# Channel sums of the q and k norms by way of HBM, roots on GpSimd, value transposes in pairs: an attention and convolution kernel on one Trainium2 core

## Chip, cores, metric

The kernel runs on one NeuronCore of a Trainium2 chip. The metric is the device time of one launch in microseconds. Three runs of the kernel before gave 3830.28, 3835.93 and 3836.73 us, so the median is 3835.93 us. All data is float32.

## What is computed

The input x has 48 channels of 256 x 256 pixels. Two layers follow each other, each added to its input after a group norm. The first is attention over 4 x 4 patches, the second a sum of three small matrix products along width, height and channel within 64 x 64 windows. The change touches the first:

```python
qkv = jnp.einsum('bchw,oc->bohw', gn(x), w_qkv)
qkv = dwconv3x3(qkv, w_dw)
q, k, v = jnp.split(qkv, 3, axis=1)
q, k, v = (heads(q), heads(k), heads(v))   # unfold in 4x4 patches, 8 heads
q = q / max(sqrt(sum(q*q, axis=-2)), 1e-12)   # the sum runs over 96 = 6 channels x 16 pixels
k = k / max(sqrt(sum(k*k, axis=-2)), 1e-12)
attn = softmax(einsum('bhcn,bhcm->bhnm', q, k) * temperature)
out = einsum('bhcn,bhnm->bhcm', v, attn)
```

A head has 96 values for each of 4096 patches (plus border patches, which are zero and enter as a constant in the softmax sums). A patch's norm takes the squares of 6 channels and 16 pixels.

## The kernel before

Engines are named as in the profile: PE is TensorE, DVE VectorE, ACT ScalarE, POOL GpSimd, SP SyncE.

**Stages.** First x is loaded and its group statistics are taken. The 1x1 convolution of heads 0 and 1 follows (`pointwise`), then the depthwise convolution and norms of head 0 (`depthwise_first`). Then comes the attention of heads 0 to 7, in which the depthwise part of head h+1 runs beside the attention of head h. The projection and the second layer end the kernel. A branch for large temperatures (line 465) is not taken with these inputs.

**The attention loop** (lines 607 to 690) is under a manual schedule, so each engine issues its instructions in the order of the program text. For each head h there are 16 steps g, called stages here, and in each stage four steps k. A stage computes two blocks of 128 rows of scores (`scores`: 24 PE products of 512 columns and four exponentials on ACT for each block), normalises them on DVE (`normalised`: four small operations that end in the scaled value tile vn), and weighs the values with them (`weigh`, line 563: four groups of products, k = 0 to 3). Each group is added to the accumulator oacc by DVE (line 581). Scores, weighted sums and the strips named below take turns in three PSUM tiles named big.

**The depthwise rows.** In stages g = 0 to 11 of heads 0 to 6, ten rows r = 0 to 9 of the next head pass through (`Depthwise`, line 199). A tile has 126 partitions: 7 chunks of the image times 18 channels (6 each of q, k and v). Row d = g - 1 is handled thus in stage g. DVE runs taps 1 to 3 after the first `normalised`, taps 4 to 8 after the second (`tap`, line 234). ACT squares the result (`square`, line 245). At k=0 DVE sums the 16 pixels (`reduce`, line 249, result ss, 126 x 64). At k=2 a PE product with a 0/1 matrix named same adds the 6 channels of a group and leaves the sum in each of their partitions (`norm`, line 253, result pn in PSUM), and DVE computes the inverse root of it by an integer guess and three Newton steps, twelve operations in all (`root`, lines 257 to 274, result y; q rows are multiplied by the temperature, v rows become 1). At k=3 DVE multiplies the row by y (`scale`, line 279, result o).

In the following stage the row is p = g - 2. POOL stores o, ACT rounds o to oh, POOL subtracts to get ol (`low`, line 292), and POOL stores both (line 297). Row n = g gets its first tap on ACT (`first`, line 215). In head 0 each step k also has a strip of the 1x1 convolution of heads 2 to 7 (`Strip`: a load, four PE products, one ACT pass, two stores).

**SP's queue** issues, in the order of the text: values and keys of the next head, the queries of stage g+2, in head 0 the strips' loads and stores, and at k=2 the `pad` tile of row g+1.

**Value transposes.** In stages g = 11 to 14 of heads 0 to 6, `load_value` fetches two value tiles of the next head through SP (two buffers vt). `turn` (line 521) transposes one tile by four PE transposes into a PSUM tile pst, and ACT copies it to vT. One turn is at k=0, the other at k=2. pst shares two PSUM buffers, tag "one", with pn and with the output transposes pt.

Of the kernel before, what the change touches and what calls it, by code (L numbers as in the profile page):

```python
# [8 lines left out]
F32 = mybir.dt.float32  # L9
F32R = mybir.dt.float32r  # L10
AF = mybir.ActivationFunctionType
ALU = mybir.AluOpType
AX = mybir.AxisListType
# [16 lines left out]
CR = 9  # L30
HC = 3 * C // NH
NP1 = CH * HC
PX = W // KS
# [10 lines left out]
def conv_preact_kernel(  # L44
# [15 lines left out]
    nc = tc.nc  # L60
# [4 lines left out]
    dram = ctx.enter_context(tc.tile_pool(name="dram", bufs=1, space=DRAM))  # L65
# [6 lines left out]
    CN = CR * PX  # L72
    t1 = [dram.tile([(h1 - h0) * HC, TR, W + 2], F32, name=f"t1_{h0}") for h0, h1 in GROUPS]
    qkv = [dram.tile([3, CH, HC * KK, CN + PX], F32, name=f"qkv{h}") for h in range(NH)]
    os_ = dram.tile([C * KK, NT], F32, name="os_")
    x1s = dram.tile([C, H, W], F32, name="x1s")

# [15 lines left out]
    for s in range(2):  # L93
        r = slice(s * C, (s + 1) * C)
        for h in range(NH if s == 0 else H0):
            o = s * M0 + h * HC if h < H0 else (h - H0) * HC
            nc.scalar.dma_start(
                out=(wq[r] if h < H0 else wr[0:C])[:, o : o + HC].rearrange("c (z e) -> c z e", z=3),
                in_=w_qkvT.rearrange("c (z h e) -> h c z e", z=3, h=NH)[h],
# [4 lines left out]
    for z in range(3):  # L104
        for j in range(CH):
            p = j * HC + z * 6
# [23 lines left out]
    nmul = const.tile([NP1, NH], F32, name="nmul")  # L130
    nadd = const.tile([NP1, 1], F32, name="nadd")
# [65 lines left out]
    class Depthwise:  # L197
# [53 lines left out]
        def norm(self):  # L251
            self.pn = one.tile([NP1, PX], F32, name="pn", tag="one")
            nc.tensor.matmul(self.pn, lhsT=same, rhs=self.ss, start=True, stop=True)  # L253

        def root(self, on_scalar=False):
            n = self.pool.tile([NP1, PX], F32, name="n", bufs=2)
            nc.vector.tensor_scalar_max(n, self.pn, 1e-24)
            y = self.pool.tile([NP1, PX], F32, name="y", bufs=2)
            if on_scalar:
                nc.scalar.activation(n, n, AF.Sqrt)  # L260
                nc.vector.reciprocal(y, n)
                nc.vector.tensor_scalar(y, y, nmul[:, self.h : self.h + 1], nadd, ALU.mult, ALU.add)
                self.y = y
                return

            nc.vector.tensor_scalar(
                y.bitcast(mybir.dt.int32), n.bitcast(mybir.dt.int32), -0.5, 1597463007.0, ALU.mult, ALU.add
            )
            z = self.pool.tile([NP1, PX], F32, name="z", bufs=self.bufs)
            for _ in range(3):  # L270
                nc.vector.tensor_mul(z, y, y)
                nc.vector.scalar_tensor_tensor(z, z, -0.5, n, ALU.mult, ALU.mult)
                nc.vector.scalar_tensor_tensor(y, z, 1.5, y, ALU.add, ALU.mult)
            nc.vector.tensor_scalar(y, y, nmul[:, self.h : self.h + 1], nadd, ALU.mult, ALU.add)
            self.y = y
# [112 lines left out]
    with tc.tile_pool(name="xn", bufs=1) as xnp, tc.tile_pool(name="cst", bufs=1) as cst, tc.tile_pool(  # L388
        name="nps", bufs=2, space=PSUM
# [9 lines left out]
        for j in range(0, HALF, LR):  # L399
            for s in range(2):  # L400
                eng = nc.sync if s == 0 else nc.scalar
                eng.dma_start(
                    out=xr[s * C : (s + 1) * C, j : j + LR, :], in_=xc[:, s * HALF + j : s * HALF + j + LR, :]
# [8 lines left out]
        for g, (w, k) in enumerate(((wq, P2), (wr, C))):  # L412
            m = w.shape[1]
# [51 lines left out]
    with tc.If(nc.values_load(large) > 0):  # L465
# [8 lines left out]
        with tc.tile_pool(name="mk", bufs=NM) as mk, tc.tile_pool(name="mq", bufs=2) as mq, tc.tile_pool(  # L474
            name="mps", bufs=2, space=PSUM
# [23 lines left out]
    with tc.tile_pool(name="ahead", bufs=2) as ah, tc.tile_pool(name="ae", bufs=3) as ae, tc.tile_pool(  # L499
        name="asm", bufs=6  # L500
# [6 lines left out]
        def load_key(h, m, eng=nc.sync):  # L507
            keys[h, m] = ah.tile([128, 2, 512], F32R, name="kt", bufs=14)
            load_keys(keys[h, m], h, m, eng)

        def load_query(h, g):
            queries[h, g] = ah.tile([128, 3, 256], F32R, name="qt", bufs=2)
            load_queries(queries[h, g], h, g)

        def load_value(h, m):

            vt = ah.tile([HD, 4 * 128], F32, name="vt")
            load(vt, qkv[h][2, :, 2 * HD :], m * 512, (m + 1) * 512)
            values[h, m] = vt

        def turn(h, m):
            ps = one.tile([128, 4, HD], F32, name="pst", tag="one")
            for i in range(4):
                nc.tensor.transpose(ps[:, i, :], values[h, m][:, i * 128 : (i + 1) * 128], ident[:HD, :HD])  # L524
            vT = ah.tile([128, 4, HD], F32, name="vT", bufs=9)
            nc.scalar.copy(vT, ps)
            values[h, m] = vT
# [79 lines left out]
        with tc.manual_schedule():  # L607
            load_query(0, 1)
            block = scores(0, 0)
            for h in range(NH):  # L610
                more = h + 1 < NH
                rows = {r: Depthwise(h + 1, r) for r in range(CR + 1)} if more else {}
                for g in range(NG):
                    p, d, n = rows.get(g - 2), rows.get(g - 1), rows.get(g)

                    if h == 0 and 0 < g <= 6:
                        load_value(0, g + 1)
                    if more and CR + 2 <= g < CR + 6:
                        for m in range(2):
                            load_value(h + 1, (g - CR - 2) * 2 + m)  # L620
                    if more and CR + 3 <= g < CR + 6:
                        for m in range(2):
                            load_key(h + 1, (g - CR - 3) * 2 + m)

                    blocks = [normalised(*block)]
                    block = scores(h, g * G + 1)
                    if more and g == NG - 1:
                        load_key(h + 1, 6)
                        load_key(h + 1, 7, nc.gpsimd)
                    if g + 2 < NG:  # L630
                        load_query(h, g + 2)
                    elif more:
                        load_query(h + 1, g + 2 - NG)
                    if p:
                        p.store((2,))
                    if d:
                        for t in range(1, 4):
                            d.tap(t)
                    second = block
                    if g + 1 < NG:  # L640
                        block = scores(h, (g + 1) * G)
                    elif more:
                        block = scores(h + 1, 0)
                    blocks.append(normalised(*second))
                    if d:
                        for t in range(4, 9):
                            d.tap(t)

                    if g == 0 and rows:
                        rows[0].load()  # L650
                    if p:
                        p.high()
                    if d:
                        d.square()
                    if n:
                        n.first()
                    for k in range(NK):
                        s = (h * NG + g) * NK + k
                        weigh(h, g, blocks, k)
                        if k == 0 and d:  # L660
                            d.reduce()
                        if k == 0 and p:
                            p.low(nc.gpsimd)
                            p.store((0, 1))
                        for w in strips[s]:
                            w.run(big.tile([128, 2, 512], F32, name="big"))
                        for w in strips[s + 2]:
                            w.load()
                        for w in strips[s - 1] if s else []:
                            w.store()  # L670
                        if k == 2 and d:
                            d.norm()
                            d.root()
                        if k == 2 and g + 1 in rows:
                            rows[g + 1].load()
                        if k == 3 and d:
                            d.scale()
                        if h == 0 and 0 < g <= 6 and k == 0:
                            turn(0, g + 1)
                        if more and CR + 2 <= g < CR + 6 and k in (0, 2):  # L680
                            turn(h + 1, (g - CR - 2) * 2 + k // 2)

                        if g == 0 and h > 0 and k == 0:
                            for m in range(6, 8):
                                store(h - 1, m)
                        if g == NG - 1 and k > 0:
                            for m in range(2 * k - 2, 2 * k):
                                store(h, m)
            for m in range(6, 8):
                store(NH - 1, m)  # L690
# [6 lines left out]
    with tc.tile_pool(name="pj", bufs=3) as pj, tc.tile_pool(name="pjs", bufs=1) as pjs, tc.tile_pool(  # L697
        name="pps", bufs=3, space=PSUM
# [47 lines left out]
        for s in range(2):  # L746
            nc.scalar.dma_start(
                out=csn[s * 64 : s * 64 + C].rearrange("c (t d) -> c t d", t=T3), in_=Cs.rearrange("t c d -> c t d")
# [11 lines left out]
    with tc.tile_pool(name="lx", bufs=2) as lx, tc.tile_pool(name="lz", bufs=2) as lz, tc.tile_pool(  # L760
        name="lr", bufs=2
    ) as lr, tc.tile_pool(name="ly", bufs=4) as ly, tc.tile_pool(name="ps1", bufs=2, space=PSUM) as ps1, tc.tile_pool(
        name="ps2", bufs=2, space=PSUM
# [162 lines left out]
```

## Time and profile before

| | |
|---|---|
| median of three runs | 3835.93 us |
| the profiled execution | 3845.87 us |
| its span | 3844.1 us |
| mean granted TensorE clock | 0.959 |
| PE busy | 3525.9 us |
| DVE busy | 2199.1 us |
| ACT busy | 1717.9 us |
| POOL busy | 583.3 us |
| pn products (line 253), two passes for each of 80 rows | median 274 ns a pass |
| roots on DVE (lines 271 to 273), 630 operations of 126 x 64 | 225 ns each |
| o (line 279), the multiplication by y | 75 of 1992 ns, 5 of 1221 ns |

How to read it: the span is the time from the first to the last instruction of one profiled execution. An engine's busy time is the sum of its instructions over the whole span. A group's line gives the source line, engine, operation, output and inputs with their shapes and count, the busy sum and the mean of one in ns, and after a second bar the idle time of the engine just before these instructions and what ended most of it. In a timeline, the first column is the start in us, the second the duration, and the bracket at the end is idle time before it. In the chain of waits, a row is a piece of the path that ended last. For DMA issues, the last number is the median time from issue to landing where it is known; SP's issues have none.

### The profile page before, as it was taken

The page shows a single profiled execution, that of the slowest core. Times are in us where ns is not written, and L with a number is a line of the kernel's source. Part 1 is how long each engine was busy: PE and PEld are TensorE (multiplying, and loading weights), DVE is VectorE, ACT ScalarE, POOL GpSimd, SP SyncE. Part 2 cuts the span into 40 slices and gives each one's busy share as a digit, 9 for nine tenths or more (in the row PEclk, how much of TensorE's full clock was granted, in tenths as well). Part 3 has the DMA queues.
Part 4 walks back from the last instruction along what each step waited for, and adds up shares of the span by engine and source line. Part 5 has one row for each costly group of instructions (what it writes and reads, how often), then busy time and mean ns, then how long its engine had stood idle before and what let it go on. Part 6 is the DMA issues. An engine that isn't in the chain of part 4 may idle for free.

```text
span 3844.1 us, 99863 instructions
## 1 busy us (share of the span) xinstructions
PE 3525.9 (92%) x44216; PEld 2927.6 (76%) x44216; DVE 2199.1 (57%) x3520; ACT 1717.9 (45%) x2668; POOL 583.3 (15%) x535
## 2 busy tenths in 40 slices
PE   1856999999999999999999999999999999755998
PEld 0324777788888888888888888888888888514776
DVE  5562776169727962994399359826972222365553
ACT  0223565555545544554455455545554444200222
POOL 0150212012201220221022112201220000000111
PEclk9877999999999999999999999999999999866999
DMA  6475676534523443444244325433542000598555
GB/s 142 153 163 144 178 196 179 175 109 117 119 81 101 119 110 87 104 120 98 83 117 115 94 81 128 111 88 92 128 113 75 24 18 22 116 238 141 111 105 100
DMA packets 280235, 441.66 MB, mean 115 GB/s; under 512 B 57354, under 2 KB 205082, under 8 KB 276336
## 3 DMA queue, kind: packets, MB, share of 16 engines
q1 hardware_dynamic: 225150, 260.52, 26.7%
q0 software_dynamic: 48896, 165.90, 19.2%
q10 hardware_dynamic: 5746, 8.73, 1.0%
q8 instruction: 351, 5.75, 0.6%
q14 instruction: 92, 0.75, 0.1%
HBM read 234.76 MB, written 199.95 MB: 113 GB/s over the span
## 4 chain that ended last, share of the span: by engine, by line
PE 73%; issue 10%; DMA 8%; DVE 2%; SPq 1%; POOL 0%; ACT 0%; POOLq 0%; ACTq 0%; DVEq 0%
PE big L339 32%; PE big L570 31%; DMA lxq<-x1s 3%; PE pb L826 3%; PE pa L804 2%; PE big L183 2%; DMA pot<-os__70 2%; PE pc L843 1%; DMA qkv<-o 1%; DMA pxt<-in_x_dram 1%; PE pst L524 1%; PE pt L587 1%; PE pn L253 1%; DMA xs<-in_x_dram 1%; DMA kt<-qkv 1%
## 5 line engine op out<-in xcount | busy, mean ns | idle before, releaser
L541 ACT ACTIVATE e<-big,nmx 128x1024 f32<-128x1024 f32 x1024 | 1144.0, 1117 | 846.2 <-PE big L339 636.4
L339 PE MATMUL big<-kt,qt 128*128 128x512 f32 x6144 | 1441.9, 394 | 57.9 <-DMA kt<-qkv 54.9
L570 PEld LDWEIGHTS big<-vn,e 128*64 128x64 f32 x32768 | 1364.8, 137 | 87.7 <-ACT e L541 45.1
L570 PE MATMUL big<-vn,e 128*64 128x96 f32 x32768 | 1422.7, 248 | 9.1 <-ACT ot L186 4.0
L339 PEld LDWEIGHTS big<-kt,qt 128*128 128x128 f32 x6144 | 1147.9, 189 | 322.0 <-issue 63.1
L581 DVE TENSOR_TENSOR oacc<-big,oacc 128x768 f32<-128x768 f32 x480 | 458.2, 955 | 708.7 <-PE big L570 708.7
L234 DVE SCALAR_TENSOR_TENSOR acc<-pad,dwt,acc 126x1024 f32<-126x1024 f32 x600 | 779.3, 1300 | 34.2 <-ACT acc L215 18.5
L292 POOL TENSOR_TENSOR ol<-o,oh 126x1024 fp32r<-126x1024 f32 x80 | 189.9, 2373 | 909.1 <-DVE ss L249 810.1
L554 DVE TENSOR_REDUCE zt<-zs 128x1 f32<-128x4 f32 x256 | 38.8, 152 | 368.5 <-ACT e L541 368.5
L811 DVE TENSOR_TENSOR lzt<-pa,cbias 128x864 f32<-128x864 f32 (+1 forms) x88 | 136.3, 1621 | 134.5 <-PE pa L804 134.5
L541 ACT ACTIVATION_READ_ACCUMULATOR e<-big,nmx 128x1 f32 x1024 | 196.3, 192 | 0.0
L833 ACT COPY lyt<-pb 128x512 f32<-128x512 f32 x144 | 84.3, 586 | 250.0 <-PE pb L826 250.0
L297 POOL DMA_DIRECT2D qkv<-o x80 | 101.0, 1262 | 567.8 <-DVE zu L556 348.7
L245 ACT ACTIVATE sq<-acc 126x1024 f32<-126x1024 f32 x75 | 79.3, 1058 | 171.7 <-issue 111.6
L279 DVE TENSOR_TENSOR o<-acc,y 126x1024 f32<-126x1024 f32 x75 | 149.4, 1992 | 11.0 <-DMA qkv<-o 11.0
L826 PEld LDWEIGHTS pb<-wsb,lzt 128*64 128x64 f32 x2304 | 132.1, 143 | 28.1 <-issue 21.1
L715 PE MATMUL pps<-pot,wp 96*96 96x512 f32 x128 | 77.9, 778 | 77.6 <-DMA pot<-os__70 77.6
L826 PE MATMUL pb<-wsb,lzt 128*64 128x128 f32 x2304 | 147.9, 287 | 1.3 <-issue 1.3
L186 ACT ACTIVATE ot<-big,bias 108x1024 f32<-108x1024 f32 x64 | 71.0, 1112 | 147.8 <-PE big L183 68.2
L804 PE MATMUL pa<-csn,lxq 48*128 48x144 f32 x1024 | 95.1, 333 | 33.9 <-DMA lxq<-x1s 32.6
L590 POOL DMA_DIRECT2D os__70<-oo x64 | 32.6, 514 | 615.4 <-ACT oo L589 615.4
L715 PEld LDWEIGHTS pps<-pot,wp 96*96 96x96 f32 x128 | 26.9, 218 | 128.0 <-issue 126.4
(115 smaller groups left out, 1897.6 us busy)
## 6 DMA issues: line engine op xcount, KB each, us to landing
pad<-t SPq DMA_DIRECT2D x80, 761.9 KB
qkv<-o POOLq DMA_DIRECT2D x80, 504.0 KB, 6.9
qkv<-oh POOLq DMA_DIRECT2D x80, 504.0 KB, 7.4
qkv<-ol POOLq DMA_DIRECT2D x80, 504.0 KB, 9.1
t<-ot SPq DMA_DIRECT2D x128, 217.7 KB
qt<-qkv SPq DMA_DIRECT2D x176, 96.0 KB
xs<-in_x_dram SPq DMA_DIRECT2D x128, 96.0 KB
os__70<-oo POOLq DMA_DIRECT2D x64, 192.0 KB, 2.8
```

What stands on the lines that cost most here:

```text
L234: nc.vector.scalar_tensor_tensor(self.acc, self.pad[:, dy : dy + KS, dx : dx + W], dwt[:, self.h, tap : tap + 1], self.acc, ALU.mult, ALU.add,
L279: nc.vector.tensor_tensor(self.o.rearrange("p (a b) x -> p a b x", a=KS), self.acc.rearrange("p a (x b) -> p a b x", b=KS), self.y.rearran ...
L292: eng.tensor_sub(self.ol, self.o, self.oh.bitcast(F32))
L297: nc.gpsimd.dma_start(out=qkv[self.h][i].rearrange("j (c k) n -> (j c) k n", k=KK)[:, :, px], in_=self.o if i == 2 else (self.ol if i else ...
L339: nc.tensor.matmul(ps[:, i, :], lhsT=qt[:, r, q0 : q0 + 128], rhs=kts[2 * j + i][:, r // 2, :], start=(r == 0), stop=(r == 2),)
L541: nc.scalar.activation(e[:, j * 1024 : (j + 1) * 1024], ps.rearrange("p a b -> p (a b)"), AF.Exp, bias=nmx[:, b : b + 1], accum_out=zs[:, ...
L570: nc.tensor.matmul(ps[p : p + 64, j // 4, j % 4 * HD : (j % 4 + 1) * HD], lhsT=e[:, mb * 128 + p : mb * 128 + p + 64], rhs=vn, start=(i == 0),
L581: nc.vector.tensor_add(oaccs[h, k], ps[:, :, : 4 * HD], oaccs[h, k])
L715: nc.tensor.matmul(ps[:, i : i + 2, :], lhsT=wp, rhs=ot[:, ki * KS + i : ki * KS + i + 2, :], start=True, stop=True,)
L804: nc.tensor.matmul(pa[:, s, i * T3 * C : (i + 1) * T3 * C], lhsT=xq[r, y0 + i, :], rhs=csn[r], start=True, stop=True,)
L811: nc.vector.tensor_tensor(zv[:, :, y0 : y0 + n, :], pa[:, :, : n * T3 * C].rearrange("p s (y k) -> p s y k", y=n), cbias.rearrange("p (u v ...
L826: nc.tensor.matmul(pb[s * WS : (s + 1) * WS, i, :], lhsT=zts[u][:, t * C + c + i, :], rhs=wsb[:, t, :], start=True, stop=True,)
```

## The change

Three things are changed in the attention loop; `depthwise_first` and the branch for large temperatures keep `norm` and `root`.

1. `norm` is replaced by `gather`, at k=0 after the strips' work: SP writes ss to one of two HBM tiles, then reads it back into sg so that each partition of a group of 6 gets the rows of all 6 channels.
2. `root` is replaced by `root_beside` at k=2: DVE adds the six rows of sg to n, and POOL runs the bound and the inverse root in sixteen operations.
3. Both turns of a stage stand at k=0.

In the class, n and y get as many buffers as the pool gives, one in the attention loop.

```diff
--- before.py
+++ after.py
@@ -72,6 +72,7 @@
     CN = CR * PX
     t1 = [dram.tile([(h1 - h0) * HC, TR, W + 2], F32, name=f"t1_{h0}") for h0, h1 in GROUPS]
     qkv = [dram.tile([3, CH, HC * KK, CN + PX], F32, name=f"qkv{h}") for h in range(NH)]
+    ssd = [dram.tile([NP1, PX], F32, name=f"ssd{i}") for i in range(2)]
     os_ = dram.tile([C * KK, NT], F32, name="os_")
     x1s = dram.tile([C, H, W], F32, name="x1s")
 
@@ -252,10 +253,39 @@
             self.pn = one.tile([NP1, PX], F32, name="pn", tag="one")
             nc.tensor.matmul(self.pn, lhsT=same, rhs=self.ss, start=True, stop=True)
 
+        def gather(self):
+
+            to = ssd[self.r % 2]
+            nc.sync.dma_start(out=to, in_=self.ss)
+            self.sg = self.pool.tile([NP1, 6, PX], F32, name="sg")
+            nc.sync.dma_start(
+                out=self.sg,
+                in_=to.rearrange("(g u c) n -> g u (c n)", u=1, c=6).to_broadcast([NP1 // 6, 6, 6 * PX]),
+            )
+
+        def root_beside(self):
+
+            n = self.pool.tile([NP1, PX], F32, name="n", bufs=min(self.bufs, 2))
+            nc.vector.tensor_reduce(n, self.sg.rearrange("p c n -> p n c"), AX.X, ALU.add)
+            y = self.pool.tile([NP1, PX], F32, name="y", bufs=min(self.bufs, 2))
+            z = self.pool.tile([NP1, PX], F32, name="z", bufs=self.bufs)
+            nc.gpsimd.tensor_scalar_max(n, n, 1e-24)
+            nc.gpsimd.tensor_scalar(
+                y.bitcast(mybir.dt.int32), n.bitcast(mybir.dt.int32), -0.5, 1597463007.0, ALU.mult, ALU.add
+            )
+            nc.gpsimd.tensor_scalar_mul(n, n, -0.5)
+            for _ in range(3):
+                nc.gpsimd.tensor_mul(z, y, y)
+                nc.gpsimd.tensor_mul(z, z, n)
+                nc.gpsimd.tensor_scalar_add(z, z, 1.5)
+                nc.gpsimd.tensor_mul(y, z, y)
+            nc.gpsimd.tensor_scalar(y, y, nmul[:, self.h : self.h + 1], nadd, ALU.mult, ALU.add)
+            self.y = y
+
         def root(self, on_scalar=False):
-            n = self.pool.tile([NP1, PX], F32, name="n", bufs=2)
+            n = self.pool.tile([NP1, PX], F32, name="n", bufs=min(self.bufs, 2))
             nc.vector.tensor_scalar_max(n, self.pn, 1e-24)
-            y = self.pool.tile([NP1, PX], F32, name="y", bufs=2)
+            y = self.pool.tile([NP1, PX], F32, name="y", bufs=min(self.bufs, 2))
             if on_scalar:
                 nc.scalar.activation(n, n, AF.Sqrt)
                 nc.vector.reciprocal(y, n)
@@ -668,17 +698,19 @@
                             w.load()
                         for w in strips[s - 1] if s else []:
                             w.store()
+                        if k == 0 and d:
+                            d.gather()
                         if k == 2 and d:
-                            d.norm()
-                            d.root()
+                            d.root_beside()
                         if k == 2 and g + 1 in rows:
                             rows[g + 1].load()
                         if k == 3 and d:
                             d.scale()
                         if h == 0 and 0 < g <= 6 and k == 0:
                             turn(0, g + 1)
-                        if more and CR + 2 <= g < CR + 6 and k in (0, 2):
-                            turn(h + 1, (g - CR - 2) * 2 + k // 2)
+                        if more and CR + 2 <= g < CR + 6 and k == 0:
+                            for m in range(2):
+                                turn(h + 1, (g - CR - 2) * 2 + m)
 
                         if g == 0 and h > 0 and k == 0:
                             for m in range(6, 8):
```

With the schedule of the loop, DVE's order in such a stage is: taps, sum k=0, ss, sums k=1 and k=2, n, sum k=3, o, and then the next stage's `normalised` and taps. POOL's order is: the store of the row before's o, ol, the stores of oh and ol, the sixteen operations. SP's order is: the queries, in head 0 the strip of k=0, the write of ss, the read of sg, and at k=2 the pad. All but two of the sixteen operations wait for the completion of POOL work before them; the first one waits for DVE's n.

## Prediction

> **What bounds the kernel now.** I read the page's shares of busy time first, then the chain of work that ended last cut to the attention part, then the timelines of DVE, GpSimd (POOL) and SP over one stage. A "stage" is one pass of the g loop; head 1 and later are taken where strips are done.
>
> ```profile
> PE 3525.9 (92%) x44216; PEld 2927.6 (76%) x44216; DVE 2199.1 (57%) x3520; ACT 1717.9 (45%) x2668; POOL 583.3 (15%) x535
> ```
> DVE looks half idle, but that is a mean over stages of different kinds. The chain inside a stage that carries a depthwise row:
>
> ```profile
> 1636.32 8.07 PE big L570 x192
> 1644.40 0.36 PE pn L253 x2
> 1644.76 2.79 PE big L570 x64
> 1647.55 11.10 PE big L339 x48
> ```
> TensorE does not wait: 8.07 + 0.36 + 2.79 + 11.10 = 22.3 us per stage, of which the norm's product is 0.36. The same stage on DVE:
>
> ```profile
> 1618.33 0.95 DVE L581 TENSOR_TENSOR oacc<-big,oacc 128x768 f32<-128x768 f32 x1
> 1619.59 1.22 DVE L249 TENSOR_REDUCE ss<-sq 126x64 f32<-126x1024 f32 x1 [0.31 <-ACT sq L245]
> ...
> 1622.99 0.21 DVE L257 TENSOR_SCALAR n<-pn 126x64 f32<-126x64 f32 x1
> ...
> 1626.04 0.95 DVE L581 TENSOR_TENSOR oacc<-big,oacc 128x768 f32<-128x768 f32 x1
> 1626.91 1.99 DVE L279 TENSOR_TENSOR o<-acc,y 126x1024 f32<-126x1024 f32 x1
> ...
> 1634.18 6.56 DVE L234 SCALAR_TENSOR_TENSOR acc<-pad,dwt,acc 126x1024 f32<-126x1024 f32 x5
> 1640.66 0.95 DVE L581 TENSOR_TENSOR oacc<-big,oacc 128x768 f32<-128x768 f32 x1
> ```
> From one k=0 sum (1618.33) to the next (1640.66) DVE takes 22.33 us, and all its marked idle is 0.31 + 0.45 us. It is as full as TensorE, and runs in program order. So a wait put into DVE here has 0.8 us of cover plus whatever DVE work the change removes.
>
> **What the skill says.** (1) GPSIMD Engine Reference, section 3.1 (Elementwise): a two-input op costs about 2.6 cycles of 1.2 GHz per element, 2.17 ns, beside a dispatch. Agrees: the row below has 1024 elements in 2373 ns, so about 2.22 us plus 0.15 fixed. (2) DMA: Bandwidth & Descriptors, section Anatomy of one DMA: a DMA costs about 2.0 us fixed, mostly the receipt of the last write, heaviest into HBM. Agrees: 36 KB into HBM landed after 2.1 us. (3) Perfetto Trace Analysis, GPSIMD Engine Instruction: POOL's spans are unreliable and should be timed by spacing of starts. Memsets here show it: spans 0.11 us, spacing 0.03.
>
> ```profile
> L292 POOL TENSOR_TENSOR ol<-o,oh 126x1024 fp32r<-126x1024 f32 x80 | 189.9, 2373 | 909.1 <-DVE ss L249 810.1
> L365 POOL TENSOR_SCALAR diag<-ident,dwt 126x126 f32<-126x126 f32 x9 | 5.3, 598 | 0.0
> t<-zr POOLq DMA_DIRECT2D x2, 36.3 KB, 2.1
> kt<-qkv POOLq DMA_DIRECT2D x7, 192.0 KB, 3.0
> ```
>
> **Part by part.** The new path runs in 70 stages (7 heads, rows 0 to 9).
>
> *Removed.* The pn product, 0.36 us of TensorE in each: 70 x 0.36 = 25 us, a real saving only while TensorE sets the stage. On DVE the twelve root operations, 1622.99 to 1626.04, 3.05 us per stage.
>
> *Added on DVE.* One reduction of 384 elements to 64 per partition. The ss reduction takes 1217 ns for 1024, so about 0.5 us (0.4 to 0.6).
>
> *Added on SP, the gather.* After ss, SP writes ss (32 KB) to HBM, waits for its landing, and reads it back six-fold (126 rows of 1536 B, 194 KB). Nearest rows: 2.1 and 3.0 us, so g = 5.1 us from the end of ss to sg. Low 3.7 (the 20 KB wr copy's 1.7 plus the skill's 2.0), high 6.7 (3.0 for the write, 3.7 of the 128 KB kt row for the read, with the oh and ol stores running beside it). Queued behind it on SP: the pad of the next row (now at +0.2 us after the taps, then about +5, needed some 23 us later, hidden) and, in the next stage, queries and values, issued 10 us later: hidden. With head 0's strips SP is busier; see below.
>
> *Moved to POOL: the roots.* Sixteen dependent ops of 64 elements: 9 two-input, 7 scalar. By the rows: two-input 64 x 2.17 ns + 0.14 fixed = 0.28; scalar, spacing 0.585 for 126, less 0.14, gives 3.5 ns per element, so 0.37. 9 x 0.28 + 7 x 0.37 = 5.1, plus 14 waits between them at 0.035 (DVE's dependent ops start every 0.26 for 0.225 of work), P = 5.6 us. No trace row has such a small POOL op, so the bounds are wide: 0.2 each (3.2 us) to 0.6 each (9.6 us). They also stand behind work on POOL: low 2.36 us, two store issues 2.5, free 5.0 us after ss.
>
> *The added waits.* First, n waits for sg on DVE; behind it stands the k=3 sum, whose PSUM tile TensorE needs three chunks later. Second, scale waits for y from POOL; behind it stand both vn groups and all eight taps. Nothing covers this wait: between n and scale DVE has only the k=3 sum.
>
> *New length of a stage.* From the k=0 sum to the end of ss 2.48 (1618.33 to 1620.81); gather and n 5.1 + 0.5 = 5.6, by then POOL is free (5.0); roots 5.6 (the k=3 sum, 0.95, lies beside them); from scale to the next k=0 sum 13.75 (1626.91 to 1640.66). Sum 27.4 us against 22.33, so +5.1, although DVE itself is busy 2.5 us less. TensorE without pn would need 21.97 and is now the one that waits.
>
> *Over a head.* Ten rows have nine such intervals; the tenth is followed by a stage without taps, where TensorE is held only by the late k=3 sum, about 1.5 us. At entry TensorE has some play: now its first product starts 4.4 us before the k=0 sum (1613.93), and in the new rhythm 6.5, as it waits for the second vn, just ahead of five taps. Together 9 x 5.1 + 1.5 - 2.1 = 45 us; six heads, 272 us.
>
> *Head 0.* Its strips make a stage 27.28 us (405.36 to 432.64), with 5.5 us of DVE idle:
>
> ```profile
> 409.43 0.96 DVE L581 TENSOR_TENSOR oacc<-big,oacc 128x768 f32<-128x768 f32 x1 [1.64 <-PE big L570]
> 413.26 0.96 DVE L581 TENSOR_TENSOR oacc<-big,oacc 128x768 f32<-128x768 f32 x1 [2.88 <-PE big L570]
> 414.65 0.22 DVE L257 TENSOR_SCALAR n<-pn 126x64 f32<-126x64 f32 x1 [0.44 <-PE pn L253]
> ```
> The same sum, 2.4 + g + 0.5 + 5.6 + 14.1, is 28.1 with g = 5.5 (strip traffic), +0.8. SP issues in most of this stage, and a gather that holds its queue for 2 us delays strip loads, on which one wait of 10.64 us is already in the chain; I put 1 us per stage on this. 10 x 1.8 = 18 us; from -4 to +60.
>
> *Transposes.* Eight per pair at k=0 in place of four at k=0 and four at k=2: same count, TensorE time unchanged, in stages without roots. The pn tile no longer shares the two PSUM buffers. The second value tile must have landed 5 us earlier; SP has the whole of the previous stage for it. I cost it at nothing; if that cover were gone, about 1 us in each of 28 stages, 28 us.
>
> *Sum.* 272 + 18 = +290 on the profiled execution of 3845.9 us (span 3844.1): 4136. The median of the runs lies 10 us lower, so 4126, rounded to 4125.
>
> **Rivals.**
> - *Cheaper roots* (0.2 us each, P = 3.2): stage 25.0, +2.7; 6 x (24.3 - 0.6) = 142, head 0 hidden: about 3978. For it: a pipelined POOL, as the memsets; against: a wait between nearly all of them.
> - *Dearer roots* (0.5 each, P = 8): stage 29.8, +7.5; 6 x 66.9 + 25 = 426: about 4262. For it: the scalar row's 0.6 us for just 126 elements, and an integer form no row prices. A g of 7.5 us does the same.
> - *Faster: all of it hides*, place DVE's scale. If roots end within 21.97 - 2.48 - 13.75 = 5.7 us of ss, TensorE keeps setting the stage and 25 us come off: 3811. As POOL is free only at 5.0, the sixteen roots would have to take under 0.7 us, 0.045 each. Memsets space at 0.03, but those do not depend on each other.
> - *The paired transposes cost or give something*: within 28 us, no sign of its own.
>
> **How the numbers follow.** Likeliest case (roots 0.28 to 0.42, about 4030 to 4200) 0.47; cheaper roots 0.24; dearer roots or gather 0.22, a quarter of it above 4300; hidden 0.04; a change below 0.2% 0.03 (0.2%, 8 us, is about what a measurement of this kernel can tell from no change). The extreme corners are 3944 and 4464; the range 3950 to 4300 leaves out the hidden cases, the tail above and a little of the cheap roots.
>
> **What would show it.** In the new profile DVE's n waits 2 to 4 us for a DMA, o waits about 4 to 5 us for POOL's y; the interval of k=0 sums is near 27 us in heads 1 and later and near 28 in head 0; TensorE idles on DVE (vn, oacc) in those stages; stages without rows stay at 22 to 23 us. Wrong if y comes before the k=3 sum ends, if POOL's roots space under 0.1 us, or if TensorE still has no gap.

## The result, and the profile after

The changed kernel takes 4279.91 us (median of five runs, 4257.91 to 4282.81) against 3834.44 us: 1.114 times as long, interval 1.112 to 1.117. The profiled execution took 4257.91 us, with a span of 4255.8; it is the fastest of the five, and where the others spend up to 25 us more no trace shows. What follows accounts for the profiled one. The added lines shift the numbers: the taps are L235, oacc is L611, o is L309, the weighing products L600.

The shares of busy time first:

```profile
PE 3639.0 (86%) x44076; PEld 3014.0 (71%) x44076; DVE 2074.9 (49%) x2750; ACT 1713.6 (40%) x2668; POOL 954.9 (22%) x1655
```

DVE has 124 us less to do than before, and the kernel is 412 us longer. The share of busy time says nothing of this. The timeline of DVE, here over one stage, does:

```profile
1803.44 0.95 DVE L611 TENSOR_TENSOR oacc<-big,oacc 128x768 f32<-128x768 f32 x1
1804.70 1.22 DVE L250 TENSOR_REDUCE ss<-sq 126x64 f32<-126x1024 f32 x1 [0.31 <-ACT sq L246]
...
1807.40 0.96 DVE L611 TENSOR_TENSOR oacc<-big,oacc 128x768 f32<-128x768 f32 x1 [0.62 <-PE big L600]
1810.96 0.84 DVE L269 TENSOR_REDUCE n<-sg 126x64 f32<-126x384 f32 x1 [2.60 <-DMA sg<-ssd]
1811.72 0.95 DVE L611 TENSOR_TENSOR oacc<-big,oacc 128x768 f32<-128x768 f32 x1
1818.38 2.00 DVE L309 TENSOR_TENSOR o<-acc,y 126x1024 f32<-126x1024 f32 x1 [5.71 <-POOL y L282]
...
1825.65 6.56 DVE L235 SCALAR_TENSOR_TENSOR acc<-pad,dwt,acc 126x1024 f32<-126x1024 f32 x5
1832.12 0.95 DVE L611 TENSOR_TENSOR oacc<-big,oacc 128x768 f32<-128x768 f32 x1
```

From one k=0 sum to the next it now takes 28.68 us, against 22.33. Two waits have appeared: 2.60 us for sg, 5.71 for y (in heads 1 to 6 the medians are 3.37 and 5.70). SP's side of the first, with issue times:

```profile
1805.94 0.32 SPq L259 DMA_DIRECT2D ssd<-ss  x1
1807.37 0.80 SPq L261 DMA_DIRECT2D sg<-ssd  x1
```

The read waits for the write, and went out 1.43 us after the write's issue, so the write had landed by then. The read was there 3.59 us later (n at 1810.96). TensorE in the same stretch:

```profile
1809.91 11.27 PE L369 MATMUL big<-kt,qt 128*128 128x512 f32 x48
1821.28 0.39 PE L600 MATMUL big<-vn,e 128*64 128x96 f32 x4
1825.79 12.21 PE L600 MATMUL big<-vn,e 128*64 128x96 f32 x252 [4.12 <-DVE vn L590]
```

It starts to weigh, and waits for the second vn, which stands behind o and three taps in DVE's order. The chain of waits for the stage before that one, with most of POOL's sixteen pieces left out:

```profile
1776.68 1.41 DMA ssd<-ss
1778.10 4.14 DMA sg<-ssd
1782.27 0.84 DVE n L269
1783.19 0.38 POOL n L272
...
1789.24 0.41 POOL y L282
1789.67 2.01 DVE o L309
1792.44 1.20 DVE acc L235
```

Before, all pieces of the chain in such stages were TensorE's.

By the starts of ss, in us:

| | before | after |
|---|---|---|
| head 0, first ss to last ss | 254.0 | 289.3 |
| heads 1 to 6, first to last ss, mean | 202.2 | 265.2 |
| last ss of a head to the first of the next, heads 1 to 5, mean | 161.4 | 162.9 |
| a usual interval, heads 1 to 6 (after: 40 of 54) | 22.3 | 28.4 to 29.3 |

So the loss sits in the stages with a depthwise row, and the stretches without one are nearly as they were.

### The profile page after: what moved, and what is told of

The parts are those of the page before. It is cut to its first block, busy times and chain, and to the rows that moved or that the text cites. A ratio compares the mean times of both kernels' runs of the same rounds, so it can differ in the third digit from the quotient of the medians.

```text
span 4255.8 us, 100220 instructions
## 1 busy us (share of the span) xinstructions
PE 3639.0 (86%) x44076; PEld 3014.0 (71%) x44076; DVE 2074.9 (49%) x2750; ACT 1713.6 (40%) x2668; POOL 954.9 (22%) x1655
## 4 chain that ended last, share of the span: by engine, by line
PE 33%; issue 20%; DMA 16%; DVE 13%; POOL 7%; ACT 3%; SPq 1%; ACTq 0%; POOLq 0%; DVEq 0%
PE big L369 14%; PE big L600 12%; DMA sg<-ssd 6%; DVE acc L235 5%; DMA ssd<-ss 3%; DVE o L309 2%; PE pb L858 2%; DMA lxq<-x1s 2%; DVE ss L250 2%; PE pa L836 2%; ACT sq L246 2%; DMA pxt<-in_x_dram 1%; POOL z L280 1%; POOL z L279 1%; POOL y L281 1%
## 5 line engine op out<-in xcount | busy, mean ns | idle before, releaser
L600 PE MATMUL big<-vn,e 128*64 128x96 f32 x32768 | 1512.0, 256 | 220.5 <-DVE vn L590 209.0
L600 PEld LDWEIGHTS big<-vn,e 128*64 128x64 f32 x32768 | 1460.5, 144 | 314.5 <-DVE vn L590 220.2
L369 PE MATMUL big<-kt,qt 128*128 128x512 f32 x6144 | 1487.6, 400 | 143.4 <-DVE oacc L611 69.4
L369 PEld LDWEIGHTS big<-kt,qt 128*128 128x128 f32 x6144 | 1164.7, 192 | 437.8 <-DVE oacc L611 88.9
L235 DVE SCALAR_TENSOR_TENSOR acc<-pad,dwt,acc 126x1024 f32<-126x1024 f32 x600 | 779.2, 1300 | 34.1 <-ACT acc L216 18.3
L611 DVE TENSOR_TENSOR oacc<-big,oacc 128x768 f32<-128x768 f32 x480 | 456.2, 954 | 682.9 <-PE big L600 682.9
L309 DVE TENSOR_TENSOR o<-acc,y 126x1024 f32<-126x1024 f32 x75 | 150.3, 2004 | 397.7 <-POOL y L282 385.1
L269 DVE TENSOR_REDUCE n<-sg 126x64 f32<-126x384 f32 x70 | 58.2, 832 | 235.7 <-DMA sg<-ssd 235.6
L343 POOL DMA_DIRECT2D kt<-qkv x28 | 14.7, 529 | 547.9 <-PE big L369 547.8
```

The lines of the kernel that those rows point to most:

```text
L235: nc.vector.scalar_tensor_tensor(self.acc, self.pad[:, dy : dy + KS, dx : dx + W], dwt[:, self.h, tap : tap + 1], self.acc, ALU.mult, ALU.add,
L309: nc.vector.tensor_tensor(self.o.rearrange("p (a b) x -> p a b x", a=KS), self.acc.rearrange("p a (x b) -> p a b x", b=KS), self.y.rearran ...
L369: nc.tensor.matmul(ps[:, i, :], lhsT=qt[:, r, q0 : q0 + 128], rhs=kts[2 * j + i][:, r // 2, :], start=(r == 0), stop=(r == 2),)
L600: nc.tensor.matmul(ps[p : p + 64, j // 4, j % 4 * HD : (j % 4 + 1) * HD], lhsT=e[:, mb * 128 + p : mb * 128 + p + 64], rhs=vn, start=(i == 0),
L611: nc.vector.tensor_add(oaccs[h, k], ps[:, :, : 4 * HD], oaccs[h, k])
```

## Experiments

Two explanations stood against each other. The first, called the theory here: two waits stand in DVE's order, and the stage is as long as the walk from ss through HBM, POOL and the taps. The rival: the added transfers, SP's longer queue, or TensorE's clock (0.928 granted in the mean, 0.959 before) cost the time. Runs of the kernel before in the same series had medians of 3836.7 to 3840.1 us.

**Roots back on DVE, gather kept.**

```diff
-            nc.gpsimd.tensor_scalar_max(n, n, 1e-24)
+            nc.vector.tensor_scalar_max(n, n, 1e-24)
...
-                nc.gpsimd.tensor_mul(z, y, y)
-                nc.gpsimd.tensor_mul(z, z, n)
-                nc.gpsimd.tensor_scalar_add(z, z, 1.5)
-                nc.gpsimd.tensor_mul(y, z, y)
+                nc.vector.tensor_mul(z, y, y)
+                nc.vector.scalar_tensor_tensor(z, z, -0.5, n, ALU.mult, ALU.mult)
+                nc.vector.scalar_tensor_tensor(y, z, 1.5, y, ALU.add, ALU.mult)
```

> Roots back on DVE (twelve operations, 3.05 us), gather through HBM kept. Theory of the wait chain: a stage in heads 1 to 6 is 2.48 to the end of ss, about 6.3 for gather and n, 3.05 roots, 0.9 for the k=3 sum that now follows them, 13.75 from scale to the next k=0 sum: 26.5 us against about 29.2, so 9 x 6 x 2.7 = 146 us come off, 4280 to about 4130. Rival, that the added transfers, SP's queue and a lower TensorE clock cost the time and the roots' place does not: within 20 us of 4280.

Measured: 4131.26 us, 1.077 times before (1.074 to 1.080); intervals mostly 26.0 to 26.7 us. The theory's 26.5 and 4130 hold.

```profile
1758.35 0.84 DVE L269 TENSOR_REDUCE n<-sg 126x64 f32<-126x384 f32 x1 [3.95 <-DMA sg<-ssd]
...
1762.25 0.95 DVE L609 TENSOR_TENSOR oacc<-big,oacc 128x768 f32<-128x768 f32 x1
1763.12 2.00 DVE L307 TENSOR_TENSOR o<-acc,y 126x1024 f32<-126x1024 f32 x1
```

Here o has no idle time before it. DVE does the roots itself and is busier than in the changed kernel (2257.2 us against 2074.9), and the stage is shorter.

**Product back, roots kept on POOL.**

```diff
-            nc.vector.tensor_reduce(n, self.sg.rearrange("p c n -> p n c"), AX.X, ALU.add)
+            nc.vector.tensor_scalar_max(n, self.pn, 1e-24)
...
-                        if k == 0 and d:
-                            d.gather()
                         if k == 2 and d:
+                            d.norm()
                             d.root_beside()
```

> Channel sum back as a TensorE product, no transfers through HBM, roots on GpSimd kept (fifteen operations; DVE takes the bounded sum from PSUM). Theory: n is there 4.9 us after the k=0 sum, but GpSimd is busy until 2.48 + 5.05 = 7.5 with ol and two store issues; roots 6.1, then 13.75: 27.4 us per stage, 5.1 over before, 9 x 6 x 5.1 = 275, head 0 mostly hidden by its idle time: about 4110. Rival (transfers, queue and clock): back to within 40 us of before, 3835 to 3875.

Measured: 4074.0 us, 1.062 (1.059 to 1.066); intervals 27.2 us, and head 0 back at 251.9. The roots' place alone, without one added transfer, costs 236 us, over half of the loss. The time is 36 us under the theory's; the stage length was right within 0.2, so it is the sum over a head that was set too high.

**The transfers alone, on the kernel before.**

```diff
+                        if k == 0 and d:
+                            d.gather()
                         if k == 2 and d:
                             d.norm()
                             d.root()
```

> The kernel before with both transfers of the gather issued at their place in SP's queue, and nobody reading what they bring; sum by product, roots on DVE, turns at k=0 and k=2. Theory: in heads 1 to 6 nothing waits, so stages stay at 22.3; in head 0 the strips' loads stand behind the wait for the write, at most 3 us in each of ten stages: 3835 to 3870. Rival (transfers, queue and clock carry the 445 us): above 4000.

(n and y keep the changed kernel's one buffer.) Measured: 3878.58 us, 1.011 (1.008 to 1.013), a little above the upper end. In heads 1 to 6 every interval is as before (22.2 to 22.6, 23.6 for the first). What the loop loses is in head 0, 282.6 us instead of 254.0 from first to last ss. There the chain of waits runs through the gather and the strips behind it in SP's queue (L178 issues their loads, L196 their stores):

```profile
408.94 2.17 DMA ssd<-ss
411.13 0.81 SPq L261
...
412.04 0.41 SPq L178
...
413.39 11.91 DMA t<-ot
```

So the traffic costs nothing in heads 1 to 6, and the gather costs about 29 us where strips stand behind it in the queue. How much of this is the hold of the queue, and how much a slower landing of the strips' own transfers, the run does not separate.

**Paired turns alone, on the kernel before.**

```diff
-                        if more and CR + 2 <= g < CR + 6 and k in (0, 2):
-                            turn(h + 1, (g - CR - 2) * 2 + k // 2)
+                        if more and CR + 2 <= g < CR + 6 and k == 0:
+                            for m in range(2):
+                                turn(h + 1, (g - CR - 2) * 2 + m)
```

> The kernel before with both turns of a stage at k=0 and nothing else. Theory: no change, 3834 within 8 us, as the count of transposes stays and the tiles have landed. Rival: the second tile comes late, up to 1 us in each of 28 stages, up to 3862; or a gain of some us from fewer switches.

Measured: 3831.95 against 3837.99, 0.998 (0.997 to 0.999): a small gain. Per head the profile has 362.3 us in place of 363.6, so 1.3 us for four stages. In the kernel before, the chain of such a stage has two sets of transposes and three runs of weighing products:

```profile
1770.28 2.79 PE big L570 x64
1773.08 0.48 PE pst L524 x4
1773.56 5.43 PE big L570 x128
1778.99 0.48 PE pst L524 x4
1779.47 2.79 PE big L570 x64
```

That is 11.97 us. With pairs, the chain of a like stage has one set of eight and two runs:

```profile
1781.26 2.79 PE big L570 x64
1784.05 0.81 PE pst L524 x8
1784.86 8.07 PE big L570 x192
```

That is 11.67 us. Of the 0.30 saved, 0.15 is in the weighing (8.07 against 5.43 + 2.79) and 0.15 in the transposes (0.81 against twice 0.48). So each run of products of one kind costs about 0.15 us more than its products add.

**One Newton step in place of three** (the inverse roots are less exact; eight POOL operations are left out).

```diff
-            for _ in range(3):
+            for _ in range(1):
                 nc.gpsimd.tensor_mul(z, y, y)
```

> The changed kernel with one Newton step in place of three (the inverse roots are then less exact; eight operations of sixteen are left out on GpSimd). Theory: GpSimd's chain is on the path one for one, eight operations at 0.41 spacing, 3.3 us per stage in heads 1 to 6: 54 x 3.3 = 177 off, and some 10 to 20 in head 0: 4280 to about 4090, o's wait for y falls from 5.7 to about 2.4 us. Rival (transfers, queue, clock): within 20 us of 4280.

Measured: 4090.02 us, 1.066 (1.063 to 1.069), as the theory said in sum; intervals mostly 25.3 to 26.4. In the profiled executions all of the gain is in heads 1 to 6 (27.5 us each from first to last ss), and head 0 has none of its 10 to 20. The wait of o, in this kernel:

```profile
1796.23 2.00 DVE L309 TENSOR_TENSOR o<-acc,y 126x1024 f32<-126x1024 f32 x1 [2.44 <-POOL y L282]
```

5.71 has become 2.44, 3.27 less for eight operations at 0.41: in these heads POOL's chain is paid one for one.

**Cover for both waits: n and the roots behind the k=3 sum, o and its store in the following stage, between taps 5 and 6.**

```diff
-                        if k == 2 and d:
-                            d.root_beside()
...
                         if k == 3 and d:
-                            d.scale()
+                            d.root_beside()
...
-                        for t in range(4, 9):
+                        for t in range(4, 6):
                             d.tap(t)
+                    if p:
+                        p.scale()
+                        p.store((2,))
+                    if d:
+                        for t in range(6, 9):
+                            d.tap(t)
```

> The changed kernel with the two waits given cover: n and the roots after the k=3 sum, and the multiplication by y in the following stage between its taps 5 and 6; the store of o follows it there. Same transfers, same GpSimd operations. Theory: DVE needs about 20 us per stage and waits for nothing, TensorE sets 21.97, 0.36 less than before: 54 x 0.36 = 19 us off in heads 1 to 6; in head 0 SP's queue still holds the strips behind the gather, 0 to 35 us: 3815 to 3850. Rival (transfers, queue, clock): above 4000.

Measured: 4100.34 us, 1.068 (1.065 to 1.071). The theory missed by some 250 us: the time is above 4000, where the rival had put it, though the trace gives another reason. Intervals are mostly 25.4 to 26.7. DVE of this kernel, and four of POOL's operations:

```profile
1768.24 3.92 DVE L235 SCALAR_TENSOR_TENSOR acc<-pad,dwt,acc 126x1024 f32<-126x1024 f32 x3
...
1772.84 2.60 DVE L235 SCALAR_TENSOR_TENSOR acc<-pad,dwt,acc 126x1024 f32<-126x1024 f32 x2
1779.01 2.08 DVE L309 TENSOR_TENSOR o<-acc,y 126x1024 f32<-126x1024 f32 x1 [3.57 <-POOL y L282]
```

```profile
1768.34 1.40 POOL L276 TENSOR_SCALAR n<-n 126x64 f32<-126x64 f32 x1
1769.71 1.28 POOL L278 TENSOR_TENSOR z<-y 126x64 f32<-126x64 f32 x1
1771.07 1.27 POOL L279 TENSOR_TENSOR z<-z,n 126x64 f32<-126x64 f32 x1
...
1776.92 0.29 POOL L278 TENSOR_TENSOR z<-y 126x64 f32<-126x64 f32 x1
```

Operations that took 0.29 to 0.38 us take 1.2 to 1.4 while DVE runs taps, one for each tap of 1.3 us, and 0.29 again once DVE stands still. The sixteen need 11 us in place of 6.5, and o waits 3.57 us for them. The page GPSIMD Engine Reference of the Trainium skill, section 1 (Specifications), says that GpSimd shares its SBUF interfaces with VectorE, with contention for VectorE instructions that have two SBUF inputs (or run in a two-port mode). This trace agrees for the taps, which have two; GpSimd's own one-input operations are stretched too (1.40 us for n). The other wait was not covered either: with the k=3 sum in front of it, n still waits 2.84 us for sg in this stage. So one cover was too short, and the other was the wrong work to hide behind.

**The same, with the gather on POOL's queue around ol.**

```diff
-            nc.sync.dma_start(out=to, in_=self.ss)
+            nc.gpsimd.dma_start(out=to, in_=self.ss)
...
                         if k == 0 and p:
                             p.low(nc.gpsimd)
+                        if k == 0 and d:
+                            d.fetch()
+                        if k == 0 and p:
                             p.store((0, 1))
```

> As the kernel with the later scale, and both transfers of the gather issued by GpSimd, the write ahead of ol and the read behind it, so that ol covers the write's landing and SP's queue is as before. Theory: head 0 is free of the queue's delay, all stages are TensorE's own: 70 x 0.36 = 25 off before, about 3810. If GpSimd's added issues (about 1 us each) reach the path, 3835 or more.

Measured: 4231.6 us, 1.102 (1.099 to 1.104). Missed: the waits were not covered to begin with (see above), and this path is longer. Its issues and their median landing:

```profile
sg<-ssd POOLq DMA_DIRECT2D x70, 189.0 KB, 3.7
ssd<-ss POOLq DMA_DIRECT2D x70, 31.5 KB, 4.6
```

The median write takes 4.6 us from POOL's queue, where SP's mostly took 1.4, and DVE waits 5.07 us for sg in the stage looked at. It is not ol alone that delays the write: that of the first row of heads 1 to 6 has no ol beside it and lands after 4.5 to 4.7 us, while most writes of head 0 land after 1.8 with ol beside them. What does is not shown. For head 0 the move did help: 274.0 us from first to last ss, against 305.3 in the run before with the gather on SP, which speaks for SP's queue as the place of that loss.

**n over neighbours** (it adds six neighbouring elements, so other numbers than the six channels).

```diff
-            nc.vector.tensor_reduce(n, self.sg.rearrange("p c n -> p n c"), AX.X, ALU.add)
+            nc.vector.tensor_reduce(
+                n, self.sg.rearrange("p c n -> p (c n)").rearrange("p (n c) -> p n c", c=6), AX.X, ALU.add
+            )
```

> The changed kernel with n summed over six neighbouring elements in place of six that lie 256 bytes apart (the sums are then of other numbers; same count of elements). If the stride makes n take 0.83 us, it falls to about 0.45 and about 20 us come off; if a fixed cost or the count does, it stays at 0.83 and the time too.

One run: 4244.55 us. n has a median of 553 ns in place of 836: the distance between the elements costs 0.28 us, a third of n. That would be 70 x 0.28 = 20 us; the time lies 13 to 38 us under the changed kernel's five, which one run does not settle.

**A full cover: o at k=2 of the next stage, the read of ss at k=2, n between taps 2 and 3; value loads and turns one stage later.**

```diff
-                    p, d, n = rows.get(g - 2), rows.get(g - 1), rows.get(g)
+                    q, p, d, n = (rows.get(g - i) for i in (3, 2, 1, 0))
...
-                        for t in range(1, 4):
+                        for t in range(1, 3):
                             d.tap(t)
+                    if p:
+                        p.root_beside()
+                    if d:
+                        d.tap(3)
...
-                        if k == 2 and d:
-                            d.root_beside()
+                        if k == 2 and d:
+                            d.fetch()
+                        if k == 2 and p:
+                            p.scale()
+                        if k == 2 and n:
+                            n.first()
```

> Both waits covered further: the write of ss at k=0, its read at k=2 ahead of the pad, n between taps 2 and 3 of the next stage, the multiplication by y at that stage's k=2, the first tap of the row after it behind that, stores a further stage later, value loads and turns one stage later (12 to 15). The last run but one of this idea showed GpSimd's roots at 1.3 us each while DVE ran taps, 0.4 otherwise. Theory: five or six roots fall on taps and the other ten run beside sums from PSUM, so y is there about 3 us after the k=0 sum, before k=2; nothing waits on DVE and TensorE sets 21.97: heads 1 to 6 lose 54 x 0.36 = 19 against before, pairing 8 more; head 0 no longer holds SP: about 3810. If DVE and GpSimd disturb each other beyond this, DVE's taps get longer than 1.30 us and the stage stays over 22.3: 3850 or more.

Measured: 3814.51 us, 0.994 (0.992 to 0.996), near the expected 3810: faster than before by 0.6%, with all the added transfers and POOL work of the change in it. Neither n nor o waits in heads 1 to 6 (median 0). The chain of waits, heads 1 to 6:

```profile
1653.77 10.71 PE big L603 x256
1664.48 11.10 PE big L372 x48
```

An interval is 21.81 us. The product in the middle of the weighing had cost 0.36 plus one break (8.07 + 2.79 = 10.86 against 10.71), 0.51 in all. A head takes 357.2 us in place of 363.6: ten times 0.51 and the pairs' 1.3. Head 0 still loses 18 us (462.7 against 444.9 from its first ss to the first of head 1). POOL of this kernel shows the two speeds side by side, on taps and then on sums:

```profile
1655.86 1.27 POOL L282 TENSOR_TENSOR z<-z,n 126x64 f32<-126x64 f32 x1
1657.22 0.37 POOL L283 TENSOR_SCALAR z<-z 126x64 f32<-126x64 f32 x1
1657.68 0.32 POOL L284 TENSOR_TENSOR y<-z,y 126x64 f32<-126x64 f32 x1
```

The last of five taps ends at 1656.95. Over the whole trace, the 378 operations of this size on POOL that start beside a tap have a median of 1.27 us, 242 beside an oacc sum (one input in PSUM) 0.33, and 131 beside ss (one input) 0.32.

**The same schedule with the product, no transfers.**

```diff
-                        if k == 0 and d:
-                            d.gather()
+                        if k == 2 and d:
+                            d.norm()
+                            d.bound()
```

> The same schedule with the channel sum by TensorE (0.36 us a stage) and no transfers through HBM; roots on GpSimd in the next stage. Theory: no wait on DVE, TensorE sets 22.33 as before, head 0 as before: 3838 less 8 of the pairs, 3830. If the roots on GpSimd slow DVE, more than 3850.

Measured: 3835.48 against 3836.73, 1.000 (0.999 to 1.001), and not the 3830 expected. (DVE takes the bounded sum from PSUM here, and n has two buffers.) Intervals are 22.3 us: the roots on POOL are free when covered, and gain nothing while TensorE still has the product. The run before, which differs in little but the way of the sum, is 21 us faster. The 8 us of the pairs are in the heads (362.3 each) but not in the time. In the profile, however, head 0 is 11 us longer than before by the measure above (456.3), though no transfer is added; so most of the 18 us of the run before need not be the gather's. Why head 0 is longer here stays open.

## Why the prediction was right in its mechanism, and where its terms were off

The direction, the two waits, their place in DVE's order and TensorE's role came out as stated; the sizes were short. The result of 4280 lies in the range, 20 us from its upper end and 155 above the likeliest value: +445 us in place of +289. The signs that it named were there: n waits (median 3.37 us, 2 to 4 forecast), o waits (5.70, 4 to 5 forecast), TensorE waits for vn, and stages without rows are as before. One stage at a time (the timelines above; for the gather all 60 rows of heads 1 to 6):

| term, us | predicted | measured |
|---|---|---|
| k=0 sum to the end of ss | 2.48 | 2.48 |
| end of ss to sg | 5.1 | median 5.3, mean 5.9 |
| n | 0.5 | 0.84 |
| roots on POOL | 5.6 | 6.5 |
| o to the next k=0 sum | 13.75 | 13.74 |
| per head, heads 1 to 6 | +45 | +63 to +64 |
| head 0 | +18 | +37 |
| sum against the profiled execution | +290 | +412 |

The gather (by its mean), n and the roots are short by 2.0 us a stage together, 18 us over nine intervals: that is the step from +45 to +63 per head. Six heads and the 19 us of head 0 make about 127, where 122 are missing. So the mis-sized terms are these three and head 0.

*Roots.* Two-input operations took 0.29 to 0.33 and scalar ones 0.37 to 0.39, near the 0.28 and 0.37 of the working; the spacing of dependent ones is 0.41, so a wait costs nearer 0.07 than the 0.035 borrowed from DVE. 0.9 us per stage.

*n.* Its price was taken from a reduction over near elements; these lie 256 bytes apart, which by the run over neighbours makes 0.28 of the 0.34 missing.

*Gather.* The parts were off in opposite ways: the write mostly 1.4 instead of 2.1, the read mostly 3.3 to 4.2 instead of 3.0. The median was nearly right because these errors cancel. Both prices came from DMAs on POOL's queue (the rows t<-zr and kt<-qkv), while the change issues on SP's. The Trainium skill's page DMA: Bandwidth & Descriptors, section Anatomy of one DMA, also gives its fixed 2.0 us for DMAs issued by GpSimd; the write from SP lies under it, and the measurement decides. And six of 60 gathers took 9 to 11 us, which the sum of medians had no place for; without them the mean is 5.4, with them 5.9. In the six the write takes 2.8 to 3.1 us and the read 6.0 to 8.1. What delays these is not shown.

*Head 0.* The gather's hold on SP was put at 1 us a stage, and it is 3: the transfers alone cost 29 us between its first and last ss, though not surely by the hold alone. The price of a queue that is full before was read from one wait, where the queue's own entries in such a stage should have been added up (in the kernel before, from 396.9 to 424.1 us, they come to 22 us).

*Pairs.* Costed at nothing, they gain 6 us (0.2%): a stage has two runs of products fewer.

*The rivals.* Dearer roots, at 0.5 each, came nearest with 4262, and for the reason of a longer path, though roots were 0.41 and the rest came from n, the gather and head 0. The hidden case fell: even 0.29 us for an operation is far from the 0.045 it asked for. The clock of TensorE fell to 0.94 and 0.88 in the stage shown and the next, which have pauses, but it is 1.00 in the stretch without rows looked at (2000 to 2144 us). In the run with the full cover, with the same transfers and POOL work but no pauses, it is 1.00 in the stages with rows too (1549 to 1745 us), so here the low clock goes with the pauses. And it costs little: in the stage shown DVE waits 0.62 us for TensorE in all, 0.45 before.

## What to carry to other kernels

Before work is moved off a full engine, ask whether that engine must wait for its result, and what stands behind the waiting instruction in its order: here DVE lost 3 us of roots and got 8.3 us of waiting. The same move pays (0.994, of which the pairs alone had 0.998) as soon as a stage of other work lies between the issue and the use; the cover must also be work that lets the helper run, since here GpSimd did one small operation per tap of DVE. And a price per stage must include the tail of its transfers and the state of the queue that they join, not the median of one.

## What the runs showed of the hardware beyond this

- GpSimd's operations on 126 x 64 float32: 0.29 to 0.39 us each, dependent ones every 0.41; 1.2 to 1.4 us beside DVE's taps, which have two SBUF inputs.
- The write of 32 KB to HBM from SP's queue mostly landed within 1.4 us of its issue (at most 3.1 in heads 1 to 6), and a six-fold read of it (189 KB) in 3.3 to 4.2 in 52 of 60 cases; the issue of the read held SP for 0.80 us, that of the write for 0.32. From POOL's queue the medians were 4.6 and 3.7.
- A DVE reduction of 384 elements to 64: 0.55 us over neighbours, 0.84 over elements 256 bytes apart.
- Breaking a run of 256 TensorE weighing products once, for a product of another kind, cost about 0.15 us beyond that product's own 0.36 (10.86 against 10.71 us).
